# A selective scan's tiles laid out channel by channel, with the gate taken where the sums leave PSUM

## The chip, the core and the metric

The kernel runs on one core of a Trainium2 chip. The metric is the device time of one execution in microseconds. The core's engines have queues of their own: PE (TensorE, matmuls), DVE (VectorE), ACT (ScalarE), POOL (GpSimd) and SP (SyncE), which here issues nearly all DMA transfers. The profile counts 16 DMA engines.

## What is computed

The reference is a chain of four layers on an image batch of 4 x 128 channels x 64 x 64: an attention layer, an adder convolution layer, a gated attention with an MLP, and a Mamba-like layer. The change touches only the end of the last one. What it has to compute, cut from the reference:

```python
def _selective_scan(u, delta, A, Bm, Cm, Dv, z):
    dA = jnp.exp(jnp.einsum('bdl,dn->lbdn', delta, A))
    dBu = jnp.einsum('bdl,bnl,bdl->lbdn', delta, Bm, u)
    ...
        h = a * h + bu            # step by step along l
    ...
    y = jnp.einsum('lbdn,bnl->bdl', hs, Cm) + Dv[None, :, None] * u
    return y * _silu(z)

y_f = _selective_scan(xs, delta, A, Bm, Cm, D_param, z)
y_b = _selective_scan(flip(xs), flip(delta), A_b, flip(Bm), flip(Cm), D_param, flip(z))
y = y_f + flip(y_b)
mamba_out = jnp.einsum('bdl,od->blo', y, out_proj_w)
x_processed = _layer_norm(mamba_out, ln_w, ln_b)
...
return f_mamba + gamma * f_low
```

There are 256 channels `d`, 16 states `n`, and 4096 positions `l` an image; the recurrence runs once forward and once backward, with the same inputs.

## The kernel before, in words

The layers run one after the other. The last one has two functions. `layer3_prepare` computes, image by image, what the scan needs and writes it to memory tensors: `delta_d`, `du_d` (delta times u), `xs_d` (u), `sz_d` (silu of z), `low_d` (the gated low part) and `xdbl_d` (rows of B and C). `layer3_scan` reads these back.

**A tile** of the scan is 8 channels by 16 states on the 128 partitions; there are 4 images x 2 halves of the channels x 16 = 128 of them. A partition stands for one pair of channel and state. So each of the 8 rows of `delta_d` and `du_d` has to stand on 16 partitions, and each of the 16 rows of B and C on 8. The DMA does this with a repeated (zero-step) dimension in its source: `by_channels` (L921 to L926) loads `dl` and `du`, half an image's positions (2048) at a time; `by_states` (L908 to L919) loads B and C once an image and half. Before, the state is the slow index: partition = 8 x state + channel.

**Order within a tile** (`piece`, L936). Eight pieces of 1024 positions: e = 0 to 3 forward, e = 4 to 7 backward. For each, ACT computes `da` = exp(delta x A) into PSUM (L945) and DVE runs the recurrence (L947, one TENSOR_TENSOR_SCAN) into a buffer `h`. `dbu`, the scan's addend, is made by POOL from `du` and B (L933), one tile ahead.

**After the scan** of a tile, `merge` (L957) adds its forward and backward `h` on PE with identity matmuls into PSUM, in 8 blocks `mg` of 512; `copied` (L967) brings each to SBUF as `m` on ACT; `times_c` (L973) multiplies by C on POOL; `sums` (L977) adds over the 16 states on PE, with a matmul of `rows_of` that puts the tile's 8 channels on 8 of 32 rows, four tiles filling one PSUM tile `y`. After each fourth tile `evacuate` (L989) copies `y` out on ACT (L994) and stores it to `y_d` (L996), with the pattern [4, 32, 512] on the memory side.

**finish** (L998) takes one block of 512 positions of an image: it loads `y_d`, `xs_d` and `sz_d` for both channel halves (L1006), forms y + 2 D u by matmuls with the identity and with `skip` (L1008, L1009), gates on DVE (L1010), multiplies by the output weights on PE (L1014), takes the layer norm (Square on ACT, the mean on PE, then the root by a logarithm and an exponential on ACT, L68 and L69; the scale on DVE, L1023; the bias and the low part on POOL, L1024 and L1025), and stores `out` (L1026). 24 of the 32 blocks are finished in the loop, one at the end of every third tile; the last image's 8 come after the loop.

**What orders the work.** The loop at L1033 writes the calls in the order wanted, and a scheduling layer turns them into one instruction stream for each engine. Each engine takes its stream in order. Buffers come from pools with a fixed number each: 6 `h`, 3 `dl`, 2 `du`, 3 `dbu`, 2 `m`, 3 of B and of C, 2 PSUM tiles for `mg`, 2 for `da`. A load into a buffer stands in SP's queue until the last reader of that buffer is through, and what is behind it in the queue stands as well.

Of the kernel before, what the change touches and what calls it, by code (L numbers as in the profile page):

```python
# [16 lines left out]
P = 128  # L17
B = 4
# [812 lines left out]
def layer3_scan(  # L831
# [9 lines left out]
    with ExitStack() as ctx:  # L841
        cp = ctx.enter_context(tc.tile_pool(name="l4c", bufs=1))
        bc = ctx.enter_context(tc.tile_pool(name="l4bc", bufs=3))
# [6 lines left out]

        of8 = cp.tile([P, ND], F32, name="of8")
        nc.vector.tensor_reduce(of8, cm.ident.rearrange("p (n d) -> p d n", d=ND), AX.X, ALU.add)
# [5 lines left out]
        for j in range(4):  # L858
            nc.vector.tensor_copy(rows_of[:, j, ND * j : ND * (j + 1)], of8)

        a = []
        for name, src in (("af", a_log), ("ab", ab_log)):
# [5 lines left out]
            for c in range(2):  # L868
                spread = sb.tile([P, D_STATE, ND], F32, tag="spread", name=f"{name}_s{c}")
                nc.vector.tensor_tensor(  # L870
                    spread,
                    t[:, c, :].unsqueeze(2).broadcast_to([P, D_STATE, ND]),
                    of8.unsqueeze(1).broadcast_to([P, D_STATE, ND]),
                    ALU.mult,
                )
                pa = ps_m.tile([P, P // ND], F32, tag="mg", name=f"{name}_p{c}")
                nc.tensor.matmul(pa, spread.rearrange("p n d -> p (n d)"), group, start=True, stop=True)
                nc.vector.tensor_copy(at[:, c, :], pa)
            a.append(at)

        d2 = cp.tile([P, 2], F32, name="d2")
        nc.sync.dma_start(d2, d_param)

        nc.vector.tensor_scalar(d2, d2, 2.0, None, ALU.mult)
        skip = cp.tile([P, 2, P], F32, name="skip")
        for c in range(2):
            nc.vector.tensor_scalar(skip[:, c, :], cm.ident, d2[:, c : c + 1], None, ALU.mult)
# [20 lines left out]
        def by_states(b, h):  # L908

            if (b, h) not in by_image:  # L910
                got = []
                for what in range(2):
                    t = bc.tile([P, HL], F32, tag="BC"[what], name=f"{'BC'[what]}{b}_{h}")
                    r = DT_RANK + D_STATE * what
                    src = xdbl_d[b, r : r + D_STATE, halves[h]]
                    nc.sync.dma_start(t, src.unsqueeze(1).broadcast_to([D_STATE, ND, HL]))
                    got.append(t)
                by_image[b, h] = got
            return by_image[b, h]  # L919

        def by_channels(src, n, h, tag, bufs):  # L921
# [3 lines left out]
            nc.sync.dma_start(t, rows8.unsqueeze(0).broadcast_to([D_STATE, ND, HL]))  # L925
            return t  # L926

        def inputs(n, h):
# [4 lines left out]
            nc.gpsimd.tensor_tensor(t, du, by_states(b, h)[0], ALU.mult)  # L933
            st[n, "dbu", h] = t

        def piece(n, e):  # L936
# [3 lines left out]
            if k == way:  # L940
                st[n, way, h] = big.tile([P, HL], F32, tag="h", bufs=6, name=f"h{n}_{way}_{h}")
# [25 lines left out]
        def copied(n, e):  # L967
            h, k = block_of(e)
            if k == 0:
                st[n, "m", h] = big.tile([P, HL], F32, tag="m", bufs=2, name=f"m{n}_{h}")  # L970
            nc.scalar.copy(st[n, "m", h][:, bass.ts(k, BK)], st.pop((n, "mg", e)))  # L971

        def times_c(n, h):  # L973
            m = st[n, "m", h]
            nc.gpsimd.tensor_tensor(m, m, by_states(tiles[n][0], h)[1], ALU.mult)  # L975

        def sums(n, h):  # L977

            j = tiles[n][2] % 4
            if j == 0:  # L980
                st["y", h] = ps_y.tile([P, BK], F32, tag=f"y{h}", name=f"y{n}_{h}")
            m = st.pop((n, "m", h))
            for g in range(4):
                nc.tensor.matmul(  # L984
                    st["y", h][32 * g : 32 * g + 32, :], rows_of[:, j, :], m[:, bass.ts(g, BK)],
                    start=(j == 0), stop=(j == 3), skip_group_check=True,
                )

        def evacuate(n, h):  # L989
            b, c, i = tiles[n]  # L990
            if i % 4 < 3:
                return
            t = sb.tile([P, BK], F32, tag="ye", name=f"ye{n}_{h}")
            nc.scalar.copy(t, st.pop(("y", h)))  # L994
            r = 8 * (i - 3)
            nc.sync.dma_start(y_d[b, c, r : r + 32, halves[h]].rearrange("r (g w) -> g r w", g=4), t)  # L996

        def finish(b, k):  # L998
# [3 lines left out]
            gated = []  # L1002
            for c in range(2):
                yx = sb.tile([P, 3, BK], F32, tag="yx", name=f"yx{v}_{c}")
                for q, src in enumerate((y_d, xs_d, sz_d)):
                    nc.sync.dma_start(yx[:, q, :], src[b, c, :, ck])  # L1006
                py = ps_m.tile([P, BK], F32, tag="mg", name=f"py{v}_{c}")
                nc.tensor.matmul(py, cm.ident, yx[:, 0, :], start=True, stop=False)  # L1008
                nc.tensor.matmul(py, skip[:, c, :], yx[:, 1, :], start=False, stop=True)  # L1009
                nc.vector.tensor_tensor(yx[:, 0, :], py, yx[:, 2, :], ALU.mult)  # L1010
                gated.append(yx[:, 0, :])
            po = ps_m.tile([P, BK], F32, tag="mg", name=f"po3_{v}")
            for c in range(2):
                nc.tensor.matmul(po, ow[:, c, :], gated[c], start=(c == 0), stop=(c == 1))  # L1014
            sq = sb.tile([P, BK], F32, tag="sq4", bufs=1, name=f"sq4_{v}")
            nc.scalar.activation(sq, po, AF.Square)
            pv = ps_m.tile([P, BK], F32, tag="mg", name=f"pvo{v}")
            nc.tensor.matmul(pv, cm.mean, sq, start=True, stop=True)  # L1018
            rs = sb.tile([P, BK], F32, tag="rs4", bufs=1, name=f"rs4_{v}")
            cm.rstd(nc, rs, pv)  # L1020
            fl = sb.tile([P, BK], F32, tag="fl", name=f"fl{v}")
            nc.sync.dma_start(fl, low_d[b, :, ck])
            nc.vector.scalar_tensor_tensor(rs, po, lw, rs, ALU.mult, ALU.mult)  # L1023
# [180 lines left out]
```

## Time and profile before

| what | value |
|---|---|
| median of 3 runs | 23555.58 us (23554.83 to 23556.7) |
| the profiled execution | 23557.55 us, span 23555.8 us |
| scan stage, first `dl` load to end of the last scan | 20211.4 to 23424.2 us |
| one scan of 1024 positions (L947) | 2349 ns |
| `da` (L945) | 1118 ns |
| `dbu` (L933), `m` times C (L975), each on 2048 positions | 4529 ns, 4522 ns |
| `m` copy (L971) | 581 ns |
| `dl`, `du` loads | 256 each, 1024 KB each |

In a group line of the profile stand the line, engine and operation, the output and inputs, the shape and count; then the busy time and the mean of one in ns; then the engine's idle time just before, and what ended most of it. The busy digits cut the span into 40 slices and give each slice's busy share in tenths. In a line for a stretch of time there is the stretch and its length, then busy time and count of PE, PEld (weight loads), DVE, ACT and POOL, the granted TensorE clock, the mean busy share of the 16 DMA engines, and what they moved in GB/s. A line of waits names who waited for whom, with the total in us, the times, and the longest.

### The profile page before, as it was taken

What the parts mean: (1) busy time and instruction counts of PE and PEld (TensorE: products, weight loads), DVE (VectorE), ACT (ScalarE), POOL (GpSimd) and SP (SyncE); (2) the same over time, 40 slices, a digit from 0 to 9 for tenths busy, and PEclk for the clock granted to TensorE, in tenths of its full rate; (3) what the DMA queues carried; (4) which work ended last, traced back from release to release, by engine and by line L of the source; (5) the groups of instructions that cost most, each with busy time, mean ns of one, the idle gap of its engine ahead of it and who ended that gap; (6) DMA issues with size and microseconds to landing.
All of it is one profiled execution on the core that took longest, in us unless ns stands there. A gap on an engine that the chain in (4) does not pass through costs nothing. (4 is left out here: it accounts for less than half of the span.)

```text
span 23555.8 us, 348033 instructions
## 1 busy us (share of the span) xinstructions
PE 21606.2 (92%) x146624; PEld 7799.2 (33%) x146624; DVE 20116.0 (85%) x15018; ACT 19647.4 (83%) x13700; POOL 3766.7 (16%) x1710
## 2 busy tenths in 40 slices
PE   9999999999999999999999999999997567677777
PEld 4443333333333333333333333333332222222222
DVE  7887999999999999889999999999997665777776
ACT  5666999999999999899999999999996336555555
POOL 5662000000000000000000000000000000577776
PEclk9999999999999999999999999999998776899999
DMA  0000000000000000000000000000000002788876
GB/s 14 9 5 12 1 3 7 1 3 5 3 3 1 3 1 3 8 5 3 5 3 1 5 5 1 3 1 3 3 1 32 0 3 96 182 195 194 194 192 163
DMA packets 174504, 809.07 MB, mean 34 GB/s; under 512 B 22716, under 2 KB 23364, under 8 KB 102788
## 3 DMA queue, kind: packets, MB, share of 16 engines
q1 hardware_dynamic: 172356, 778.42, 13.0%
q8 instruction: 1146, 18.78, 0.3%
q10 hardware_dynamic: 576, 8.39, 0.1%
q14 instruction: 426, 3.49, 0.0%
HBM read 658.15 MB, written 128.58 MB: 33 GB/s over the span
## 5 line engine op out<-in xcount | busy, mean ns | idle before, releaser
L392 ACT ACTIVATE a1a<-a1pb,a1wn 128x2048 f32<-128x2048 f32 x4096 | 7793.2, 2001 | 198.3 <-PE a1pa L338 101.3
L392 ACT ACTIVATE a2a<-a2pb,a2wn 128x2048 f32<-128x2048 f32 x4096 | 7791.9, 1999 | 136.2 <-PE a2pa L338 94.0
L403 DVE TENSOR_SCALAR a2d<-a2pb,a2wa 128x2048 f32<-128x2048 f32 x4096 | 4993.4, 1281 | 212.9 <-PE a2pa L338 212.4
L403 DVE TENSOR_SCALAR a1d<-a1pb,a1wa 128x2048 f32<-128x2048 f32 x4096 | 4992.1, 1281 | 207.2 <-PE a1pa L338 206.9
L338 PE MATMUL a2pa<-a2a,a2pick 128*32 128x512 f32 x32768 | 4576.3, 593 | 31.5 <-ACT a2a L392 31.5
L338 PE MATMUL a1pa<-a1a,a1pick 128*32 128x512 f32 x32768 | 4569.2, 593 | 31.5 <-ACT a1a L392 31.5
L338 PE MATMUL a2pa<-a2d,a2pick 128*32 128x512 f32 x32768 | 4436.8, 594 | 46.3 <-DVE a2d L403 46.0
L338 PE MATMUL a1pa<-a1d,a1pick 128*32 128x512 f32 x32768 | 4434.3, 594 | 47.2 <-DVE a1d L403 46.9
L421 DVE SCALAR_TENSOR_TENSOR a1a<-a1pb,a1wa,a1a 128x2048 f32<-128x2048 f32 x1024 | 2406.1, 2350 | 323.6 <-ACT a1a L392 323.6
L421 DVE SCALAR_TENSOR_TENSOR a2a<-a2pb,a2wa,a2a 128x2048 f32<-128x2048 f32 x1024 | 2406.1, 2350 | 314.1 <-ACT a2a L392 314.1
L338 PEld LDWEIGHTS a2pa<-a2a,a2pick 128*32 128x32 f32 x32768 | 1489.1, 110 | 2370.1 <-issue 2061.7
L338 PEld LDWEIGHTS a1pa<-a1a,a1pick 128*32 128x32 f32 x32768 | 1486.9, 110 | 2370.7 <-issue 2045.3
L962 PE MATMUL mg<-h,ident 128*128 128x512 f32 x4096 | 1982.8, 634 | 298.1 <-ACT m L971 227.4
L338 PEld LDWEIGHTS a2pa<-a2d,a2pick 128*32 128x32 f32 x32768 | 1347.1, 109 | 2472.1 <-issue 1935.5
L338 PEld LDWEIGHTS a1pa<-a1d,a1pick 128*32 128x32 f32 x32768 | 1345.4, 109 | 2471.8 <-issue 1913.8
L947 DVE TENSOR_TENSOR_SCAN h<-da,h,dbu 128x1024 f32<-128x1024 f32 x768 | 1804.2, 2349 | 87.0 <-POOL dbu L933 4.7
L962 PEld LDWEIGHTS mg<-h,ident 128*128 128x128 f32 x4096 | 787.1, 201 | 1529.4 <-issue 856.9
L186 POOL TENSOR_TENSOR ssum<-ssum,et 128x512 f32<-128x512 f32 x960 | 1230.3, 1282 | 232.9 <-ACT et L181 166.1
L975 POOL TENSOR_TENSOR m<-m,C 128x2048 f32<-128x2048 f32 x256 | 1157.7, 4522 | 605.2 <-ACT m L971 435.9
L933 POOL TENSOR_TENSOR dbu<-du,B 128x2048 f32<-128x2048 f32 x256 | 1153.6, 4529 | 26.3 <-DMA du<-du_d 26.3
L151 ACT COPY et<-pe 128x512 f32<-128x512 f32 x1024 | 596.6, 583 | 591.6 <-PE pe L149 575.9
L149 PE MATMUL pe<-q,k 128*128 128x512 f32 x2048 | 1051.1, 596 | 8.6 <-DVE mx L159 8.1
(267 smaller groups left out, 13672.1 us busy)
## 6 DMA issues: line engine op xcount, KB each, us to landing
dl<-delta_d SPq DMA_DIRECT2D x256, 1024.0 KB
du<-du_d SPq DMA_DIRECT2D x256, 1024.0 KB
xs_d<-xs SPq DMA_DIRECT2D x8, 2048.0 KB
sz_d<-sz SPq DMA_DIRECT2D x64, 256.0 KB
delta_d<-dv SPq DMA_DIRECT2D x32, 512.0 KB
du_d<-du SPq DMA_DIRECT2D x32, 512.0 KB
y_d<-ye SPq DMA_DIRECT2D x64, 256.0 KB
yx<-xs_d SPq DMA_DIRECT2D x64, 256.0 KB
```

Of the source, the lines that this page charges most:

```text
L149: nc.tensor.matmul(pe, k[:, bass.ts(j, P)], unit[u, "q"], start=True, stop=True)
L151: nc.scalar.copy(et, pe)
L186: nc.gpsimd.tensor_tensor(unit[u, "sum"], unit[u, "sum"], at, ALU.add)
L338: nc.tensor.matmul(pa[s][32 * g : 32 * g + 32, :], pick[v][:, 31 - jj : 63 - jj], d[:, bass.ts(s, BK)], start=False, stop=False, skip_grou ...
L392: nc.scalar.activation(rows(at), view(t), AF.Abs, bias=wn[t][:, co : co + 1], scale=0.5 if g == q else 1.0,)
L403: nc.vector.tensor_scalar(rows(dt), view(t), wa[:, t, co : co + 1], None, ALU.max)
L421: nc.vector.scalar_tensor_tensor(at, view(MAX_TAP), wa[:, MAX_TAP, co : co + 1], at, ALU.max, ALU.add)
L933: nc.gpsimd.tensor_tensor(t, du, by_states(b, h)[0], ALU.mult)
L947: nc.vector.tensor_tensor_scan(t[:, cols][:, s], da[:, s], st[n, "dbu", h][:, cols][:, s], 0.0 if e % 4 == 0 else st["last"], ALU.mult, AL ...
L962: nc.tensor.matmul(pm, cm.ident, st[n, way, h][:, bass.ts(k, BK)], start=(way == 0), stop=(way == 1))
L975: nc.gpsimd.tensor_tensor(m, m, by_states(tiles[n][0], h)[1], ALU.mult)
```

## The change

1. The partitions are numbered the other way round: partition = 16 x channel + state. `by_channels` and `by_states` swap the place of the repeated dimension in the source, and the small constant matrices follow (`of16`, `spread`).
2. B and C are loaded one at a time and for the next image ahead (`next_image`), with 2 buffers each in place of 3.
3. There are 7 `h` buffers for 6 and 3 `m` buffers for 2. In the loop `times_c` and `sums` come later: half 0's product with C one step later, half 1's one step later, the sums of half 0 four steps and of half 1 three steps later.
4. The skip term and the gate move from `finish` to `sums` and `evacuate`. `xs` and `sz` are loaded in the layout of `y` (pattern [4, 32, 512], new L1005), the skip is added in PSUM by 32 x 32 matmuls (new L1016), and DVE multiplies by `sz` as it takes `y` out (new L1026). `y_d` then holds gated values.
5. `finish` is a generator that is stepped through at each even step of the loop. It loads only `y_d` and `low_d` (new L1035, L1037), adds the bias to `low` on ACT (new L1039), scales on ACT (new L1045), and multiplies and adds on POOL (new L1054, L1056). `gated`, `fl` and `mo` have one buffer each.
6. The table of ACT functions that has exponential and logarithm together is loaded once ahead of the stage.

```diff
-        bc = ctx.enter_context(tc.tile_pool(name="l4bc", bufs=3))
+        bc = ctx.enter_context(tc.tile_pool(name="l4bc", bufs=2))
...
+        of16 = cp.tile([P, ND], F32, name="of16")
+        nc.vector.tensor_reduce(of16, cm.ident.rearrange("p (d n) -> p d n", d=ND), AX.X, ALU.add)
...
+        tc.keep_in_program_order(nc.scalar.preload_act_table_set("natural_log_exp_and_others"))
...
-                    nc.sync.dma_start(t, src.unsqueeze(1).broadcast_to([D_STATE, ND, HL]))
+                nc.sync.dma_start(t, src.unsqueeze(0).broadcast_to([ND, D_STATE, HL]))
...
+        def next_image(n, what, h):
+            if n % 32 == 31:
+                by_states(tiles[n][0] + 1, what, h)
...
-            nc.sync.dma_start(t, rows8.unsqueeze(0).broadcast_to([D_STATE, ND, HL]))
+            nc.sync.dma_start(t, rows8.unsqueeze(1).broadcast_to([ND, D_STATE, HL]))
...
-                st[n, way, h] = big.tile([P, HL], F32, tag="h", bufs=6, name=f"h{n}_{way}_{h}")
+                st[n, way, h] = big.tile([P, HL], F32, tag="h", bufs=7, name=f"h{n}_{way}_{h}")
...
-                st[n, "m", h] = big.tile([P, HL], F32, tag="m", bufs=2, name=f"m{n}_{h}")
+                st[n, "m", h] = big.tile([P, HL], F32, tag="m", bufs=3, name=f"m{n}_{h}")
...
+        def blocks_of(t, n, h):
+            b, c, i = tiles[n]
+            r = 32 * (i // 4)
+            return t[b, c, r : r + 32, halves[h]].rearrange("r (g w) -> g r w", g=4)
...
+            if j == 1:
+                for name, src in (("xs", xs_d), ("sz", sz_d)):
+                    t = sb.tile([P, BK], F32, tag=name, bufs=2, name=f"{name}4_{n}_{h}")
+                    nc.sync.dma_start(t, blocks_of(src, n, h))
+                    st[name, h] = t
...
+            if j == 3:
+                for g in range(4):
+                    rows32 = slice(32 * g, 32 * g + 32)
+                    nc.tensor.matmul(
+                        st["y", h][rows32, :], skip[rows32, c, q, :], st["xs", h][rows32, :],
+                        start=False, stop=True, skip_group_check=True, tile_position=(32 * g, 32 * g),
+                    )
...
-            nc.scalar.copy(t, st.pop(("y", h)))
+            t = st.pop(("sz", h))
+            nc.vector.tensor_tensor(t, st.pop(("y", h)), t, ALU.mult)
+            nc.sync.dma_start(blocks_of(y_d, n, h), t)
...
+            gated = sb.tile([P, 2, BK], F32, tag="gated", bufs=1, name=f"gated{v}")
             for c in range(2):
-                yx = sb.tile([P, 3, BK], F32, tag="yx", name=f"yx{v}_{c}")
-                for q, src in enumerate((y_d, xs_d, sz_d)):
-                    nc.sync.dma_start(yx[:, q, :], src[b, c, :, ck])
...
+                nc.sync.dma_start(gated[:, c, :], y_d[b, c, :, ck])
+            fl = sb.tile([P, BK], F32, tag="fl", bufs=1, name=f"fl{v}")
+            nc.sync.dma_start(fl, low_d[b, :, ck])
+            yield
+            nc.scalar.activation(fl, fl, AF.Identity, bias=lb)
...
+            mo = sb.tile([P, BK], F32, tag="mo", bufs=1, name=f"mo{v}")
+            nc.scalar.activation(mo, po, AF.Identity, scale=lw)
...
-            nc.vector.scalar_tensor_tensor(rs, po, lw, rs, ALU.mult, ALU.mult)
-            nc.gpsimd.tensor_scalar(rs, rs, lb, None, ALU.add)
-            nc.gpsimd.tensor_tensor(fl, rs, fl, ALU.add)
+            nc.gpsimd.tensor_tensor(mo, mo, rs, ALU.mult)
+            yield
+            nc.gpsimd.tensor_tensor(fl, mo, fl, ALU.add)
             nc.sync.dma_start(out[b, :, ck], fl)
```

The loop's part, with the calls in their new places:

```diff
+            if n >= 36 and at % 3 == 0 and at // 3 < NB:
+                steps = finish(b - 1, at // 3)
...
-                    times_c(n - 2, 0)
...
+                if e == 1 and 1 < n:
                     times_c(n - 2, 0)
+                    sums(n - 2, 1)
                 if e == 2 and 1 < n:
-                    sums(n - 2, 0)
...
+                    evacuate(n - 2, 1)
+                if e == 5 and 0 < n <= last + 1:
+                    times_c(n - 1, 1)
+                if e == 6:
+                    if n < last:
+                        inputs(n + 1, 1)
+                    if 1 < n:
+                        sums(n - 2, 0)
+                if e == 7 and 1 < n:
                     evacuate(n - 2, 0)
...
+                if e % 2 == 0:
+                    next(steps, None)
```

## The prediction

> **What bounds the kernel now.** I read the slices first, then the stretches of the scan stage, the waits inside it, and last the DMA transfers alone. Only the scan (`layer3_scan`) changes. It runs from the first `dl` load at 20211.4 us to the end of the last scan at 23424.2 us: 3212.8 us for 128 tiles, **25.1 us a tile**, with 131.6 us of tail behind it. The rest of the run keeps its instructions.
>
> ```profile
> DVE  7887999999999999889999999999997665777776
> POOL 5662000000000000000000000000000000577776
> DMA  0000000000000000000000000000000002788876
> GB/s 14 9 5 12 1 3 7 1 3 5 3 3 1 3 1 3 8 5 3 5 3 1 5 5 1 3 1 3 3 1 32 0 3 96 182 195 194 194 192 163
> ...
> POOL dbu L933 1%; POOL m L975 1%; DVE h L947 0%; PE y L984 0%; PE mg L962 0%; PE po L1014 0%; POOL rs L1024 0%; POOL fl L1025 0%; PE py L1008 0%; ACT L69 0%; PE py L1009 0%; PE pvo L1018 0%; ACT rs L68 0%; ACT L68 0%; DVE rs L1023 0%
> ...
> L947 DVE TENSOR_TENSOR_SCAN h<-da,h,dbu 128x1024 f32<-128x1024 f32 x768 | 1804.2, 2349 | 87.0 <-POOL dbu L933 4.7
> L975 POOL TENSOR_TENSOR m<-m,C 128x2048 f32<-128x2048 f32 x256 | 1157.7, 4522 | 605.2 <-ACT m L971 435.9
> L933 POOL TENSOR_TENSOR dbu<-du,B 128x2048 f32<-128x2048 f32 x256 | 1153.6, 4529 | 26.3 <-DMA du<-du_d 26.3
> ```
>
> No engine is full in the last six slices, and the DMA digit is the highest there. The chain that ended last goes round POOL, DVE and PE. The waits of DVE between 20600 and 23400 us say which of them holds the scans:
>
> ```profile
> DVE h L947 <- PE mg L962: 432.2, 222, 4.7
> DVE rs L1023 <- ACT rs L69: 200.5, 24, 10.2
> ```
>
> So the scans stand 432 us for the merges to free an `h` buffer, and 200 us behind the layer norm's L1023, of 2800 us. They stand for a DMA nowhere. Yet the transfers are near their own limit. These stretches show it; the last two columns are the share of 16 DMA engines and GB/s:
>
> ```profile
> 20211.40:23424.20 3212.80, 2493.78 (x6433) 889.31 (x6434) 2434.17 (x1109) 1819.31 (x2223) 2353.70 (x557) 0.93 0.81 192
> ...
> 20214.00:20259.00 45.00, 15.13 (x24) 5.66 (x24) 26.33 (x16) 16.85 (x18) 19.02 (x5) 0.57 1.02 221
> 20046.00:20069.50 23.50, 14.24 (x23) 5.01 (x23) 5.33 (x11) 23.21 (x31) 0.00 (x0) 0.67 1.02 234
> 17952.00:17968.00 16.00, 1.06 (x2) 0.50 (x2) 11.67 (x4) 3.62 (x1) 0.00 (x0) 0.50 1.01 431
> 23442.50:23444.40 1.90, 0.00 (x0) 0.00 (x0) 0.69 (x1) 0.00 (x0) 1.90 (x1) 1.00 0.25 92
> ```
>
> The first is the stage: share 0.81. The second holds `dl` and `du` loads alone: all engines busy at 221 GB/s, 221/(16 x 1.02) = 13.5 GB/s for each. The third holds B and C loads alone: 14.3 each. The fourth holds loads of `x` from `y2d`, with no repeated rows: 26.7 each. The fifth is one `y_d` store (L996) alone: share 0.25, 92/4 = 23 GB/s each. **Four engines of sixteen carry it.** Its small completion packets say the same:
>
> ```profile
> DMA packets 124, 0.25 MB, mean 49 GB/s; under 512 B 4, under 2 KB 4, under 8 KB 124
> ```
>
> What sets that store apart is its access pattern: [4, 32, 512] on the memory side, its slowest dimension 4. The loads with all engines have 16 (`dl`: 16 repeats of 8 rows; B: 16 rows of 8 repeats) or 128 there.
>
> **Part by part.**
>
> *The h buffers, the later sums, the m buffers.* One more `h` buffer lets the first scan of a tile wait for the merge of two tiles before, half 1, instead of half 0, and each later one likewise; this can take the 432 us. The sums and products with C move past merges in PE's queue, so PE no longer stands for POOL there.
>
> *The gate and the layer norm.* L1010 (64 x 0.67 us) and L1023 (32 x 0.75) leave DVE, with the 200 us wait; the multiply by `sz` comes back at the sums (64 x 0.67). 64 table loads of 1.28 us leave ACT's finish; two Identity activations (0.6 us each, by the row of Square) come in; 64 copies `ye` (0.58) go. POOL swaps 1.57 + 1.27 us for 2 x 1.27 a finish. PE trades 128 `py` matmuls of 128 rows for 256 of 32 rows. On engines alone, a tile would come to 8 scans at 2.43 us (three take 7.29 in a row) plus 0.33 for the gate: 19.8; POOL 4 x 4.53 + 0.6 = 18.7. Call it **20.5 us**, worth about 590 us over 128 tiles if nothing else came late.
>
> *The layout of the loads.* This is what comes late. To put 8 channels by 16 states on the partitions, the `dl` and `du` loads (4 a tile, 1 MB each) now name [8 rows, 16 repeats, 2048], and B and C [8 repeats, 16 rows, 2048]: **the slowest dimension is 8 where it was 16**. No row has an 8. By the nearest row, the 4 that got four engines, I take eight. The other end is sixteen, as now.
>
> [...]
>
> On eight engines one load is 1,048,576/8 = 131,072 bytes each. At 14.3 GB/s (the B and C stretch, whose pattern gives each engine one row to repeat, as the new `dl` has) it takes 9.17 us; at 13.5, 9.7; at 26.7, 4.91. I take 9.17, the nearest row.
>
> [...]
>
> Then a tile costs the busiest DMA engine:
> - `dl`, `du`: 4 x 9.17 = 36.7 us
> - gate: the new `xs`, `sz` loads (4 in four tiles) have slowest dimension 4, as the 2 `y_d` stores: 65,536 bytes on each of four engines at 23 GB/s = 2.85 us; 6/4 x 2.85 = 4.3. This counts them on engines that also carry `dl`. If they fell on others it is 0; if the loads ran at half rate, 7.1
> - finish: 4 transfers of 16,384 bytes an engine at 26.7 GB/s, 0.6 us each, 32 finishes: 0.6
> - B and C: 12 loads in the loop, 0.9
>
> Sum **42.4 us**, against 20.5 for the engines. The cover is gone: scans now wait for `dl`. The loads are two or three deep in the queue (3 `dl`, 2 `du` buffers), 18 to 27 us of work, so DMA hardly runs dry. One place where it does: with one `fl` buffer, SP's next `fl` load stands until the `out` store has landed, and `dl` is queued behind it on SP. The store is the last thing in the queue then. The price of an emptied queue is about one small transfer, by the chain of waits:
>
> ```profile
> 23509.90 4.94 DMA fl<-low_d
> ```
>
> 24 finishes lie in the loop: 24 x 4.9 = 118 us. In the tail the last eight finishes go one by one with that buffer; I leave the tail at 131.6 us, the table loads going and the single buffer coming.
>
> 128 x 42.4 + 118 = 5545 us, against 3212.8: +2332. The profiled execution took 23557.6 us around its span of 23555.8, 2 us over the median, so this gives **25,890 us** (+9.9%).
>
> **The rivals.**
>
> *Eight engines, at full rate.* If half rate is a matter of sixteen engines and eight do not keep it, a load takes 4.91: 19.6 + 4.3 + 0.6 + 0.5 = 25.0 us a tile, 128 x 25.0 + 118 = 3318: 23,660 us, +0.4%. Anything between is open. For it: 26.7 occurs. Against: the half rate holds in two stretches whose sources are read in quite different order (13.5 and 14.3), so it does not hang on the order of the rows.
>
> *Sixteen engines as now; faster.* If the 8 does not lower the count, a load is 65,536 bytes each, 4.58 us at 14.3: 18.3 + 4.3 + 0.6 + 0.4 = 23.6 us, still over 20.5. 128 x 23.6 + 60 (half the dry spells, as engines catch up) = 3081: 23,425 us, -0.55%. It decides as soon as a tile's transfers fall under today's 25.1. For it: dl's destination keeps 128 partitions. Against: so does the store's SBUF side.
>
> *The high end.* At 13.5 GB/s and with the gate's loads at half rate: 38.7 + 7.1 + 0.6 + 0.9 = 47.3; 6054 + 118 = 6172: 26,520 us.
>
> **How the numbers follow.** Eight engines near half rate, 25,300 to 26,520: 0.78. Eight at a higher rate, 23,660 to 25,300: 0.12, of it 0.02 at the very bottom with no change to speak of. Sixteen: 0.07 (0.06 faster, 0.01 same). Above 26,520: 0.03. 0.2% (47 us) is about what a measurement of this kernel can tell from no change. Faster 0.06, same 0.03, slower 0.91. The range 23,660 to 26,520 takes in both bounds of the load's rate; the likeliest case's own is 25,300 to 26,520.
>
> **What would show it.** A stretch of the changed scan stage with a DMA share near 0.5 or a little over, and about 115 to 130 GB/s, not 0.81 and 192; a count of small completion packets near half for `dl` and `du`; ACT's `da` and POOL's `dbu` waiting for `dl` and `du` where they now wait for DVE; PE `mg` gone as the releaser of the scans; DVE under 60% busy. A share above 0.8 would prove me wrong on the count of engines. A share of 0.5 with some 200 GB/s would prove me wrong on the rate.

## The result, and the profile after

The changed kernel takes **24300.67 us** (median of 4 runs, 24293.83 to 24324.94) against 23555.21 us before (4 runs): ratio **1.0319, 95% interval 1.0302 to 1.0335**, slower. The forecast was 25,890 us. The profiled execution took 24324.94 us around a span of 24323.1 us.

First the slices of the profiled page, each digit a fortieth of the span:

```profile
DVE  7787999999999999899999999999976655656555
POOL 5661000000000000000000000000000014655555
DMA  0000000000000000000000000000000024444444
GB/s 15 8 5 11 1 6 3 1 3 6 1 3 1 3 3 1 12 1 3 6 1 3 5 3 3 1 3 3 1 31 0 4 101 140 174 149 162 152 160 140
```

The scan stage has grown from the last six slices to the last seven, its DMA digit has halved to 4, and DVE and POOL are down to 5 and 6. The digit 4 is not slack: the stretches say so. These are the stage, 45 us early in it (87 us after its start) with `dl` and `du` loads alone, and the tail; the last two columns are again the share of 16 DMA engines and GB/s:

```profile
20213.00:24219.00 4006.00, 2517.55 (x6712) 896.90 (x6713) 2403.48 (x1100) 1734.61 (x2158) 2348.74 (x557) 0.82 0.48 156
20300.00:20345.00 45.00, 24.60 (x53) 8.27 (x52) 25.37 (x11) 15.38 (x19) 20.47 (x5) 0.77 0.51 114
24219.00:24323.00 104.00, 64.10 (x145) 20.59 (x144) 1.60 (x3) 31.43 (x50) 35.56 (x20) 0.77 0.26 81
```

4006/128 = **31.3 us a tile** (25.1 before). A share of 0.5 is what eight engines of sixteen, always busy, come to; over the whole stage the queue of the loads has 48.3%. If all of that lay on the same eight, they were idle for 3.4% of the stage, some 140 us. The engines' work is what it was (POOL 2348.74 us against 2353.70 before). The stage waits for loads. The DMA transfers of the stage alone, in packets:

```profile
DMA packets 110565, 626.31 MB, mean 156 GB/s; under 512 B 6520, under 2 KB 6520, under 8 KB 43384
```

The packets under 512 B go with the share. One `y_d` store of before, at share 0.25, has 4 of them. The loads in the first 87 us of this stage, at share 0.50, have 71 in 9.52 MB, 7.8 a load of 1 MB; those in the first 89 us of before's stage, at share 1.00, have 288 in 19.50 MB, 15.5 a load:

```profile
DMA packets 1232, 9.52 MB, mean 109 GB/s; under 512 B 71, under 2 KB 71, under 8 KB 71
```

```profile
DMA packets 2667, 19.50 MB, mean 220 GB/s; under 512 B 288, under 2 KB 288, under 8 KB 288
```

The same view of before's whole stage counts 11784 against the 6520: the bytes are nearly the same (617.13 MB), the small packets little over half. The waits between 20600 and 24100 us:

```profile
DVE h L958 <- PE mg L973: 1088.2, 197, 43.5
PE mg L973 <- ACT m L982: 1041.8, 258, 29.8
ACT da L956 <- DMA dl<-delta_d: 1028.4, 104, 36.9
...
POOL mo L1054 <- ACT rs L69: 264.9, 24, 33.4
...
POOL dbu L943 <- DMA du<-du_d: 251.5, 47, 9.2
```

ACT stands 1028 us for `dl`. The two lines above it read as the same wait seen from behind: ACT takes its queue in order, the `mg` copies (L982) stand behind the `da` that lacks its `dl`, PE finds no PSUM buffer for the next merge, and the `h` buffer that DVE needs stays taken. The wait behind L1023 of before (DVE for ACT's root, 200 us) is gone from DVE, as the change meant; POOL, which now multiplies by the root, stands 264.9 us for it.

### The profile page after: what moved, and what is told of

Same layout as the page of the kernel before. It is cut to its first block, busy times and chain, and to the rows that moved or that the text cites. A ratio compares the mean times of both kernels' runs of the same rounds, so it can differ in the third digit from the quotient of the medians.

```text
span 24323.1 us, 348426 instructions
## 1 busy us (share of the span) xinstructions
PE 21606.6 (89%) x146880; PEld 7797.8 (32%) x146880; DVE 20072.1 (83%) x14994; ACT 19552.8 (80%) x13636; POOL 3760.8 (15%) x1710
## 4 chain that ended last, share of the span: by engine, by line
PE 74%; DMA 10%; DVE 7%; ACT 4%; issue 3%; POOL 1%; SPq 0%; DVEq 0%; ACTq 0%; POOLq 0%
PE a1pa L338 29%; PE a2pa L338 29%; DMA dl<-delta_d 6%; PE pe L149 4%; PE pav L192 3%; DVE h L958 2%; DVE g L652 2%; PE mg L973 1%; PE a1pc L319 1%; PE a2pc L319 1%; DMA du<-du_d 1%; DMA y_d<-sz 1%; POOL dbu L943 1%; PE pd L637 1%; DMA out<-fl 1%
## 5 line engine op out<-in xcount | busy, mean ns | idle before, releaser
L973 PE MATMUL mg<-h,ident 128*128 128x512 f32 x4096 | 2140.0, 670 | 1486.3 <-ACT m L982 1208.8
L956 ACT ACTIVATE da<-dl,af 128x1024 f32<-128x1024 f32 x512 | 571.9, 1119 | 1383.6 <-DMA dl<-delta_d 1211.7
```

Source lines behind the costliest of these rows:

```text
L973: nc.tensor.matmul(pm, cm.ident, st[n, way, h][:, bass.ts(k, BK)], start=(way == 0), stop=(way == 1))
```

## The experiments

### Which part costs the time: e1_old_layout, e2_layout_alone, e3_gate_split

**e1** takes the layout alone back out of the changed kernel (as well as the constants that follow it):

```diff
-                nc.sync.dma_start(t, src.unsqueeze(0).broadcast_to([ND, D_STATE, HL]))
+                nc.sync.dma_start(t, src.unsqueeze(1).broadcast_to([D_STATE, ND, HL]))
-            nc.sync.dma_start(t, rows8.unsqueeze(1).broadcast_to([ND, D_STATE, HL]))
+            nc.sync.dma_start(t, rows8.unsqueeze(0).broadcast_to([D_STATE, ND, HL]))
```

> The changed kernel with the layout alone taken back (state slow, 16 repeats x 8 rows, 16 rows x 8 repeats), all its other parts kept. Theory 1 (the loads' count of engines is what made the change slower): a tile's transfers on the busiest engine are 4 x 4.6 to 4.85 + 4.3 + 0.6 + 0.4 = 23.7 to 24.7 us, the stage about 3030 to 3160 us plus some dry spells, so 23,400 to 23,570 us; DMA share in the stage 0.75 to 0.85. Rival (the new order of the calls, the gate's loads or the one fl buffer made it slower): 24,200 to 24,300 us.

Measured: 23630.61 us, ratio 1.0026 (1.0015 to 1.0037): 60 us over theory 1's range, and far from the rival's. **e2** is the reverse edit, the layout alone put into the kernel before.

> The kernel before with the layout alone changed (8 rows x 16 repeats, 8 repeats x 16 rows), nothing else. Theory 1: on eight engines at the 0.40 us a packet that the changed kernel shows, a tile takes 64 x 0.40 = 25.8 us for dl and du, 1.4 for the y_d stores, 1.2 for finish and 0.9 for B and C: 29.3 us, against 25.1 now, so 23,555 + 128 x 4.2 = about 24,090 us, share 0.5. Rival (the layout costs nothing by itself): 23,555 us.

Measured: 23946.23 us, ratio 1.0162 (1.0145 to 1.0178), 144 us under theory 1's figure. A stretch of 2400 us of each, e1 first:

```profile
20600.00:23000.00 2400.00, 1733.58 (x4886) 610.23 (x4886) 1723.00 (x782) 1254.76 (x1563) 1700.67 (x404) 0.89 0.83 191
```

```profile
20600.00:23000.00 2400.00, 1682.32 (x4217) 583.51 (x4215) 1584.41 (x715) 1183.41 (x1454) 1543.38 (x366) 0.88 0.52 168
```

With the layout out, the share is 0.83; with the layout as the only edit it is 0.52. So the layout sets the share, and without it all the rest of the change costs 0.26%. The two do not add up: 0.26% and 1.62% apart, 3.19% together. What the rest costs seems to depend on whether loads are the bound.

**e3** takes the gate's transfers (loads of `xs` and `sz`, stores of `y_d`) apart, each into four of 32 rows (the cut shows the loads):

```diff
-                    nc.sync.dma_start(t, blocks_of(src, n, h))
+                    for g in range(4):
+                        nc.sync.dma_start(t[32 * g : 32 * g + 32, :], blocks_of(src, n, h)[g])
```

> The changed kernel with each xs and sz load and each y_d store cut into four transfers of 32 rows, so that their slowest dimension is 32 in place of 4. If these transfers run on engines that also carry dl and du (theory 1): 6/4 x 2.85 = 4.3 us of a tile becomes 6/4 x 4 x 4,096 bytes / 26.7 = 0.9, so 3.4 us x 128 = 435 us less, 23,870 us; the share rises to about 0.55. If they run on other engines: no change, 24,300 us. [...]

Measured: 25105.38 us, ratio 1.0652 (1.0634 to 1.067): 800 us over the higher of the two cases, and 1235 over theory 1. SP's waits between 20600 and 23000 us, where L1006 issues the split loads, and the same stretch:

```profile
SPq L1006 <- DMA du<-du_d: 337.1, 46, 9.4
SPq L1006 <- DMA dl<-delta_d: 315.6, 51, 9.7
```

```profile
20600.00:23000.00 2400.00, 1454.47 (x3375) 484.36 (x3375) 1201.91 (x543) 863.63 (x1072) 1172.52 (x276) 0.79 0.52 130
```

SP now stands at the split loads until earlier `dl` and `du` loads have landed, so the next ones are issued late. And at the same share of 0.52, the GB/s are 130 where the changed kernel had 156: an 8 KB packet takes 0.530 us on average (mean over the trace's records of 8 KB packets in the loads' queue, here and below) against 0.403. So the time of a packet is no constant of the pattern. **e6_old_split** puts the same split on e1:

> The changed kernel with the layout of before and its gate's transfers cut into four of 32 rows each, so that no transfer is left on fewer than sixteen engines. Theory 1: 4 x 4.75 + 0.9 + 0.6 + 0.4 = 20.9 us a tile of transfers, engines 20.5: with dry spells 21.5 to 23 us a tile, 23,070 to 23,260 us, faster than both kernels. [...] Rival (more issues on SP's queue, each standing for an earlier transfer, cost what the split saves): 23,600 us as in the run with the old layout alone.

Measured: 23804.73 us, ratio 1.0106 (1.0089 to 1.0123), slower than e1 and 200 us over the rival's figure. Its packets took 0.584 us, as e1's 0.582, so their length is not the reason here. The reason that the trace offers is the waits of SP's queue (261.5 us at the split loads for `du` between 20600 and 23000 us).

### The loads by themselves: e4_loads

> Loads alone, in eight phases of 18 loads issued in a row; the rest of the computation is left out and the output is not the reference's. Phases: a = 8 rows x 16 repeats on 128 partitions (the changed kernel's dl); b = 16 repeats x 8 rows (the dl of before); c = 16 rows x 8 repeats (the B of before); d = 8 rows x 8 repeats on partitions 0 to 63; e = 8 rows x 4 repeats on partitions 0 to 31; f = 4 rows x 16 repeats on partitions 0 to 63; g = 8 blocks of 16 different rows, nothing repeated; k = 128 different rows, nothing repeated. [...] Theory 2 (repeated reads of the same rows cause the half rate): g and k are at 310 from the start, e is as slow as a. Theory 3 (the number of engines does not follow the slowest dimension): shares near 1.0 in a, d, e, f, g.

This kernel only loads. The stretches of its eight groups, a to g and then k, in order of time (the last is 128 different rows; the last two columns are share and GB/s):

```profile
10.00:170.00 160.00, 0.00 (x0) 0.00 (x0) 1.00 0.51 111
180.00:255.00 75.00, 0.00 (x0) 0.00 (x0) 1.00 1.01 222
268.00:340.00 72.00, 0.00 (x0) 0.00 (x0) 1.00 1.01 230
352.00:428.00 76.00, 0.00 (x0) 0.00 (x0) 1.00 0.51 114
440.00:455.00 15.00, 0.00 (x0) 0.00 (x0) 1.00 0.51 214
470.00:550.00 80.00, 0.00 (x0) 0.00 (x0) 1.00 0.25 105
600.00:655.00 55.00, 0.00 (x0) 0.00 (x0) 1.00 0.51 213
665.00:705.00 40.00, 0.00 (x0) 0.00 (x0) 1.00 1.01 424
```

Two things are read here. **The share follows the slowest dimension**: 8 rows x 16 repeats, 0.51; 16 x 8 in either order, 1.01; 8 x 8 and 8 x 4, 0.51; 4 x 16, 0.25; 128 rows, 1.01. In the eight groups a slowest dimension of 4 goes with a quarter of the engines' time, 8 with half, 16 and 128 with all of it; theory 3 fails.

**The rate is not a matter of repeats alone.** The first group, the changed kernel's load, runs at 111 GB/s, 0.598 us a packet, from its first to its last load; the fourth, the same on 64 partitions, stays near 0.58 as well. The fifth repeats each row four times and runs at 214, 0.309 us; it fills only 32 partitions. So repeats are not enough to make a load slow. But they have a part in whether it stays slow. The seventh writes the partitions of the first, in the same eight blocks, from 128 different rows: it begins at 0.517 us and falls to 0.310 with nothing between its loads (the stretch shows it after the fall). On sixteen engines the second and third, with repeats, stay near 0.57 to 0.60, and the eighth, without, takes 0.31 after a slow beginning (0.343 us in its first eighth).

What makes a packet long or short is not shown. The traces name no engine and no partition for a packet. The first group on 128 partitions stays at 0.598 us and the fifth on 32 is at 0.309, both at share 0.51; but the fourth and the sixth both fill 64 partitions with repeated rows, and the fourth stays near 0.58 while the sixth fell to 0.31 by itself within its first quarter.

### What lets the packets fall: e10_step, e17_even_gate, e18_alone, e19_stores, e20_no_stores

The 0.403 us of the changed kernel is the mean of a mixture: 58% of the stage's 8 KB packets take under 0.345 us, against 8% in the kernel before. From 22050 to 22064 us no `dl` or `du` packet starts. From 22064 to 22072 us they take 0.470 us, from 22076 to 22091 us 0.366, and in the end (22087 to 22100 us) 0.316, at the same share:

```profile
22064.00:22072.00 8.00, 4.70 (x8) 2.10 (x9) 2.29 (x1) 3.80 (x6) 4.18 (x1) 0.59 0.52 148
22076.00:22091.00 15.00, 12.94 (x35) 4.90 (x36) 13.14 (x6) 10.09 (x13) 7.41 (x3) 1.00 0.51 180
```

It is so over the whole stage. There are 42 spells of over 1 us in which no 8 KB packet is under way, 264 us in all; packets that start within 10 us after such a spell take 0.54 us on the mean, those that start 40 us after it or later 0.37.

Which transfer makes the packets short? **e10** puts transfers between loads of the changed form:

> Loads alone again, the rest of the computation left out and the output not the reference's: seven phases of 18 loads (8 rows x 16 repeats, the changed kernel's dl, but phase d has 16 repeats x 8 rows) with something between. a = after each third load one load of the gate's kind ([4, 32, 512], four engines); b = after each third a plain load of 128 x 512 (sixteen engines); c = after each third the same bytes as a in four loads of 32 x 512 (sixteen engines each); d = as a, among the sixteen-engine loads of the layout before; e = after each third a store of the y_d kind (four engines); f = a single load of the gate's kind after the third; g = nothing between. [...] Theory 2 (a gap or any small transfer is enough): b and c fall as a does. Theory 3 (what is in the changed kernel comes from the memory side, the two tensors read in turn, not from small transfers): all stay near 598.

Measured, 8 KB packets in the first and the last sixth of a group: with the gate's form of load after each third load 0.574 to 0.320 us; with a plain 128 x 512 load 0.596 to 0.568; with four loads of 32 rows 0.601 to 0.334; with the old layout's loads and the gate's form 0.574 to 0.489; with the store of `y_d` 0.573 to 0.310; with one load of the gate's form near the front only, 0.578 all through; with nothing, 0.585. So not only the gate's forms shorten packets, since the split loads did it as well (0.334 us; no stretch holds loads of 32 rows alone, so their sixteen engines are an estimate), and one transfer of the gate's form was not enough (0.578). Theory 2 had b fall with c, and b hardly did. **e17** asks whether the gate's transfers, [4, 32, 512], are what keeps packets short in the kernel itself, and puts them into 128 rows:

```diff
-            r = 32 * (i // 4)
-            return t[b, c, r : r + 32, halves[h]].rearrange("r (g w) -> g r w", g=4)
+            x = (8 // len(halves)) * h + i // 4
+            return t[b, c, :, bass.ts(x, BK)]
```

> The changed kernel with the gate's loads of xs and sz and its store of y_d as blocks of 128 rows x 512 instead of 32 rows x 4 x 512 (the same bytes, on sixteen engines instead of four; the gate meets other values than it should, which is the part of the computation that this changes). [...] Rival (something else keeps the packets short, and the gate's transfers only add their 4.0 us a tile): packets stay at 0.38 to 0.43 us and the kernel takes 23,800 to 24,250 us, ratio 1.010 to 1.029.

Measured: 24229.27 us, ratio 1.0276 (1.0247 to 1.0306), packets 0.430 us. The rival holds, at the edge of its range: without transfers of the gate's form the packets did not go back to the 0.57 to 0.60 us of loads alone, so that form is not what keeps them short in the kernel. Both rates stand in e17's own trace at one share:

```profile
21940.00:21990.00 50.00, 26.56 (x71) 9.54 (x69) 27.80 (x12) 18.25 (x23) 30.09 (x7) 0.83 0.50 120
21800.00:21812.00 12.00, 11.44 (x29) 4.15 (x28) 11.26 (x6) 7.41 (x10) 7.48 (x2) 0.90 0.51 205
```

**e18** tries three differences between loads alone and loads in the kernel:

> Loads of the changed kernel's form alone (8 rows x 16 repeats, 1 MB), six groups of sixteen: a back to back from one tensor; b from two tensors in turn; c with DVE and POOL at work on other tiles; d with PE and ACT at work on other tiles; e one load let in only when the load two before it has landed and been read; f the same with DVE and POOL at work. (The kernel computes nothing of the reference; it only loads.) [...] Theory T (two sources): b alone falls. If none falls, what keeps the packets at 0.40 us in the kernel stays open.

Measured, mean packet of the six groups: 0.601, 0.587, 0.591, 0.580, 0.569, 0.569 us. None falls. The work of PE and ACT came later than meant, beside the fifth group and not the fourth, and did nothing there either. The groups with two loads in flight run at a share of 0.38, not at a shorter packet. **e19** asks which of the transfers that were left makes packets short among loads alone:

> Loads of the changed kernel's form (8 rows x 16 repeats, 1 MB), five groups of sixteen, with other transfers between them: a a store of 128 rows x 512 after every second load; b a load in the form of B (8 repeats x 16 rows, 1 MB) after every fourth; c a store and a load of 128 x 512 after every second; d a store of 128 x 512 and a load on four engines (32 rows x 4 x 512); e two loads in flight at most, with a load and a store of 128 x 512 after every second. (The kernel computes nothing of the reference; it only moves data.) [...]

Measured, by eighths of each group: a, with stores of 128 x 512, from 0.581 steadily down to 0.314 us; b, with loads in B's form, 0.572 to 0.575 and 0.587 at the end; c, store and load, 0.603 to 0.314; d from 0.578 with ups between to 0.326 in the seventh eighth and 0.402 in the last; e 0.521 to 0.362, mean 0.374. Among loads alone, stores are enough. Group a's beginning and end, and group b:

```profile
5.00:40.00 35.00, 3.77 (x3) 0.00 (x0) 1.00 0.54 127
100.00:128.00 28.00, 0.00 (x0) 0.00 (x0) 1.00 0.55 210
135.00:275.00 140.00, 0.34 (x1) 0.00 (x0) 1.00 0.51 115
```

**e20** then leaves every store out of e17's scan stage:

```diff
-            nc.sync.dma_start(blocks_of(y_d, n, h), t)
...
-                nc.sync.dma_start(gated[:, c, :], y_d[b, c, :, ck])
+                nc.sync.dma_start(gated[:, c, :], xs_d[b, c, :, ck])
...
-            nc.sync.dma_start(out[b, :, ck], fl)
```

> The changed kernel with the gate's transfers in 128 rows (24,229 us) and with no store at all in the scan stage: the store of y_d and the store of out are left out (the finish reads xs_d in place of y_d, and out is filled with ones at the kernel's start, so the last layer's result is not delivered). It moves 0.5 MB less for each half of four tiles. [...] Rival (the packets stay at 0.40 to 0.45 us and only the left-out work counts): 23,900 to 24,230 us, ratio 1.014 to 1.028.

Measured: 23728.99 us, ratio 1.0076 (1.0054 to 1.0098), packets 0.384 us: shorter than e17's 0.430, not longer, and the kernel faster than even the rival said. So stores are enough among loads alone and not needed in the kernel. The kernel is 500 us faster than e17; the shorter packets account for some 64 x 0.046 x 128 = 377 us of that (64 is the number of 8 KB packets on an engine in a tile). What the stores cost besides is in part in SP's queue. In e17 this line stands between 20600 and 23000 us, in e20 there is none:

```profile
SPq L1005 <- DMA y_d<-sz: 263.6, 21, 25.9
```

### What is left when the loads are fast: e8_after_plain, e9_before_plain

Both load `dl` and `du` from 128 different rows:

```diff
-            nc.sync.dma_start(t, rows8.unsqueeze(1).broadcast_to([ND, D_STATE, HL]))
+            nc.sync.dma_start(t, src[b, c, :, halves[h]])
```

> The changed kernel with its dl and du loads taken from 128 different rows, nothing repeated: the same bytes into the same tiles in the same order, on sixteen engines at about 314 ns a packet; the values are not the ones wanted, so the output is not the reference's. Theory 1 (the loads alone hold the changed kernel back): transfers come to 4 x 2.5 + 4.3 + 0.6 + 0.4 = about 15 us a tile, the engines' 20.5 us set the pace: 20,213 + 128 x 20.5 + 105 = 22,940 us. Rival (the later sums and products, the single fl buffer or the gate cost time by themselves): over 23,400 us.

> The kernel before with its dl and du loads taken from 128 different rows in the same way; the output is not the reference's. Theory 1 (before, the merges and the layer norm hold the scans, not the transfers): 23,500 to 23,560 us, a tile at 24.7 to 25.1 us. Rival (the transfers already set part of the pace): 23,300 us or less.

e8: 23422.34 us, ratio 0.9943 (0.9924 to 0.9963). e9: 23552.82 us, 0.9997 (0.9987 to 1.0008). So the kernel before was not held by its transfers, though their share was 0.81, and the changed one, with faster loads on sixteen engines (share 0.63 between 20600 and 23000 us; half of the packets take 0.309 us or less, the mean is 0.40), gains little of what it should: its theory 1 fails, its rival holds. In e8, undisturbed tiles follow each other at 19.8 us (scans of the first piece start at 21534.8, 21554.6 and 21574.4 us). 128 of those would take 2534 us; the stage took some 3100. About **570 us** are lost. The chain of waits and then SP's own timeline at one such place (start, duration):

```profile
21605.16 10.02 DMA out<-fl
21615.19 3.34 DMA fl<-low_d
```

```profile
21605.16 0.50 SPq L1056 DMA_DIRECT2D out<-fl  x1
21611.38 0.54 SPq L1004 DMA_DIRECT2D sz<-sz_d  x1
21615.19 0.31 SPq L1036 DMA_DIRECT2D fl<-low_d  x1
21615.60 0.86 SPq L934 DMA_DIRECT2D dl<-delta_d  x2
```

SP stands some 6 us before `sz`, then 3 before `fl`, which waits for `out` to land, and only then issues `dl`.

### Can that be had back: e11_bufs, e12_plain_bufs, e13_old_bufs, e15_plain_pool

The first three add a third `sz` buffer and a second `fl` buffer, to the changed kernel, to e8 and to e1:

```diff
-                    t = sb.tile([P, BK], F32, tag=name, bufs=2, name=f"{name}4_{n}_{h}")
+                    t = sb.tile([P, BK], F32, tag=name, bufs=3 if name == "sz" else 2, name=f"{name}4_{n}_{h}")
...
-            fl = sb.tile([P, BK], F32, tag="fl", bufs=1, name=f"fl{v}")
+            fl = sb.tile([P, BK], F32, tag="fl", bufs=2, name=f"fl{v}")
```

> The changed kernel with one buffer more for the gate's sz (3 instead of 2) and for fl (2 instead of 1); nothing else moves. Theory 1 (the loads of dl and du, sixteen 8 KB packets deep on each of eight engines, set the pace: 64 packets x 0.403 us = 25.8 us of a tile's 31.3): taking away part of SP's stalls gives only what of the 31.3 us isn't covered by packets, so 24,150 to 24,310 us, ratio 1.025 to 1.032, share of the DMA engines still 0.48 to 0.52. Rival (SP's stalls behind sz, y_d and fl cost the 550 to 570 us that the kernel with 128-row loads lost): 23,700 to 23,800 us, ratio 1.006 to 1.010.

> The kernel with dl and du loaded from 128 different rows (it reads other values in the scan, so its output is not the one wanted; same bytes), with the same two buffers more. It ran 23,422 us without them, some 568 us over 128 tiles x 19.8 us. If SP's in-order stalls (fl waiting for the store of out: 53 us; sz waiting for its last reader: 107 us; both listed over 2600 us of the stage) are what makes dl late, the buffers give 150 to 350 us back: 23,070 to 23,270 us, ratio 0.979 to 0.988. If the stall only moves to the next wait of the queue (y_d's store waiting for sz, out's store waiting for POOL), it stays at 23,380 to 23,430, ratio 0.993 to 0.995.

> The changed kernel with the layout of the states taken back (16 engines, 23,631 us without the buffers, 25.9 us a tile) and the same two buffers more. If SP's stalls are the rest of the loss there: 23,350 to 23,500 us, ratio 0.991 to 0.998, a kernel faster than both. If packets are (64 packets on 16 engines at some 0.6 us are 19 to 20 us of a tile, with the gate's four-engine transfers of 4.0 us beside or behind them): 23,580 to 23,630, ratio 1.001 to 1.003.

e11: 24388.17 us, 1.0347 (1.033 to 1.0364). e12: 23400.28, 0.9933 (0.9913 to 0.9953). e13: 23603.78, 1.0019 (1.0009 to 1.0028). The buffers give 16 to 27 us at most where the loads are on sixteen engines, with intervals that overlap those of e8 and e1, and nothing in the changed kernel, which came out 78 us over the top of theory 1's range. e12's waits of SP between 20600 and 23000 us have the same names as e8's:

```profile
SPq L1056 <- POOL fl L1055: 116.4, 16, 17.3
SPq L1026 <- DVE sz L1025: 97.8, 28, 5.5
```

The `out` store waits for POOL and the `y_d` store for DVE, and no buffer takes that away. **e15** moves the `fl` load and the `out` store of e12 to POOL's queue.

> The kernel with dl and du from 128 different rows and the two buffers more (23,400 us), with the finish's load of fl and store of out issued from POOL's queue instead of SP's (the scan reads other values than it should). If SP's in-order queue is what the 550 us are (out's store and fl's load stand 10.2 and 3.4 us in the chain of waits, and dl behind them): 22,950 to 23,200 us, ratio 0.974 to 0.985. If the wait goes to another transfer of that queue (sz for y_d's store) or to POOL: 23,350 to 23,450, ratio 0.991 to 0.996.

Measured: 23539.41 us, 0.999 (0.9979 to 1.0), slower than e12 and over both ranges. The wait has moved: ACT now stands 152.3 us for `fl` between 20600 and 23000 us (17.3 in e12), and still 287.2 us for `dl` (348.8 in e12). SP's in-order queue was not all of it; where the 570 us go has not been settled.

### A version faster than both: e14_gate_in_finish, e16_finish_pool

e14 keeps the change's order (seven `h`, three `m`, later sums and products, layer norm off DVE), with the old layout, and with the gate and the skip back in `finish`, whose loads have 128 rows:

```diff
-            t = st.pop(("sz", h))
-            nc.vector.tensor_tensor(t, st.pop(("y", h)), t, ALU.mult)
+            t = sb.tile([P, BK], F32, tag="ye", name=f"ye{n}_{h}")
+            nc.scalar.copy(t, st.pop(("y", h)))
...
+                for q, src in enumerate((y_d, xs_d, sz_d)):
+                    nc.sync.dma_start(yx[:, q, :], src[b, c, :, ck])
```

> The changed kernel's order of work (products with C and sums a step later, seven buffers of h, layer norm off VectorE) with the layout of the states taken back and the gate and the skip back in the finish, where their loads have 128 rows and the sums' way out of PSUM is ScalarE's copy. If the gate at the way out of PSUM is what costs the rest (its transfers on four engines, and sz and xs queued before dl): 23,150 to 23,350 us, ratio 0.983 to 0.991, the fastest of the set. If the finish's in-order stalls are (fl, out): 23,500 to 23,650, ratio 0.998 to 1.004.

> The changed kernel's order of work with the old layout and the gate in the finish (23,319 us), with fl and out on POOL's queue. There dl was late only 83.6 us in 2400, so SP's queue has little left to give: theory 1 says 23,230 to 23,330 us, ratio 0.986 to 0.990; if POOL, which the scans wait for, pays for issuing: 23,340 to 23,500, ratio 0.991 to 0.998.

e14: **23318.88 us, 0.9898 (0.9883 to 0.9913)**, 240 us under the kernel before beside it and the fastest here that does all the work. e16, with `fl` and `out` on POOL's queue: 23466.38 us, 0.9957 (0.9941 to 0.9974), in the range of the case where POOL pays. The trace puts it otherwise: ACT stands 201.5 us for `fl` between 20600 and 23000 us, against 67.3 in e14. In e14's waits between 20600 and 23000 us, `dl` is late by 83.6 us, against e1's 476.0:

```profile
ACT da L953 <- DMA dl<-delta_d: 83.6, 26, 8.9
```

So the order of work is worth having (23.3 us a tile), and the gate at the way out of PSUM cost about 300 us (e1 against e14, by their ratios). Whether that is its transfers on four engines or their place ahead of `dl` in SP's queue, these two runs do not separate.

## Why the prediction was right in direction and wrong in size

**The step that failed** is "I take 9.17, the nearest row", the time of one `dl` or `du` load on eight engines. It carried the rate of loads on sixteen engines (14.3 GB/s for each) over to loads on eight, for the whole stage. Loads of the new form alone do run at that rate (111 GB/s on eight engines is 13.9 each, e4), and early in the stage they did (114 GB/s). The prediction chose 14.3 over 13.5 because B's pattern would give each engine one row; no trace shows which engine reads which row. Over the stage a packet took 0.403 us, so a load of 16 packets on each engine took 16 x 0.403 = **6.45 us**. The prediction's own sum with this term is 4 x 6.45 + 4.3 + 0.6 + 0.9 = 31.6 us a tile, against 31.3 measured. With each run's own packet time the sum also comes near e17 (64 x 0.430 + 2.4 = 29.9 against 30.4) and e20 (64 x 0.384 + 1.95 = 26.5 against 26.6), with 0.6 us for each 128 x 512 transfer in place of the gate's term, and e2 (64 x 0.395 + 1.4 + 1.2 + 0.9 = 28.8 against 28.5), e11 (64 x 0.418 + 5.8 = 32.6 against 32.2) and e3 (64 x 0.530 + 2.4 = 36.3 against 37.4). The packet times are read from these runs, so this shows which term was off and not why.

Point by point:

- **Eight engines**: right. The share (0.50 at the start of the stage), the small packets (7.8 a load against 15.5) and e4 (0.51 for 8 rows x 16 repeats) show it; the prediction had it as an estimate from one store's four. The rival "sixteen engines" is out.
- **The rate**: wrong, and between the two bounds, as the rival "eight engines, at full rate" left open. The argument against that rival was that half rate does not hang on the order of the rows. That is so (e4, second and third group: 222 and 230 GB/s), but the rate is no constant either: the same form takes 0.598 us a packet alone and 0.403 in the stage. Rows from late in the kernel before would have given the same price: its packets took 0.566 us on the mean over the whole scan stage, 8% of them under 0.345. The old form hardly left the slow rate in the kernels, the new one did (58%), and no row of before shows the new form.
- **The gate's term, 4.3 us**: the sum needs it, but e17, which takes the four-engine transfers away, came out only 71 us faster, since its packets were longer (0.430 us). The term by itself was not measured.
- **The engines alone, 20.5 us**: about right; e8's undisturbed tiles take 19.8. The hidden gain existed, and e14 shows 240 us of it.
- **The dry spells, 118 us**: in the changed kernel, some 140 us of idle eight-engine time by the share; by the packet records 264 us without a large load under way, part of it filled by the gate's and the finish's transfers. But once loads are fast, e8 loses about 570 us to waits of which this one is a part. This term would have sunk the fast rivals: "sixteen engines" put 23.6 us a tile, and e1, which is that case, took 25.9 (from 20213 to 23526 us).
- **The tail, 131.6 us**: it shrank to 104.
- **What would show it**: share, the count of small packets, `da` and `dbu` waiting for their loads came as said. GB/s (156, not 115 to 130) showed the rate wrong. "PE `mg` gone as the releaser" was wrong in form: DVE still stands 1088.2 us for PE `mg`, which by the reading above is ACT's wait of 1028.4 us for `dl` under another name.

**What stays open** is why packets in the kernel are 0.38 to 0.43 us. Out as the sole cause are the gate's pattern (e17) and the stores (e20). Not enough alone are other engines' work, two sources, a short queue (e18), a plain load, or B's form (e10, e19). In four kernels' traces fewer spells of over 1 us without a large load go with shorter packets: 2 and 0.384 us in e20, 25 and 0.395 in e2, 42 and 0.403 in the changed kernel, 81 and 0.530 in e3. But e17 and e11 have 42 as well, with 0.430 and 0.418, and loads issued one behind the other stay at 0.598 all through (e4). So a cause is not shown.

## What to carry to other kernels

Before a layout moves to another partition order, count the slowest dimension of each repeated load: here 16 to 8 halved the engines' share (1.01 to 0.51 in e4) and made the loads the bound (ACT stood 1028.4 us for `dl`), in a kernel whose engines had less work. A rate taken from one access pattern is not a safe price for another, even where it held for a whole stage: here the old form took 0.566 us a packet and the new one 0.403. A run of the new loads alone would have misled too (0.598 us); only with other transfers between them did they speed up. Look also at what stands ahead of large loads in an in-order queue: taking the gate's transfers away from there (e14) went with some 300 us, though moving two others to POOL's queue made things slower (e15, e16).

## What the runs showed of the hardware

Loads of 1 MB on eight engines, into the same partitions, ran at 111 GB/s with rows repeated sixteen times and, after a slow beginning, at 213 with different rows (e4, first and seventh group): 0.598 against 0.310 us for a packet of 8 KB. The slow form stays slow for 160 us of such loads alone. With stores of 128 x 512, or with loads of 32 rows, between them, packets come down to 0.31 to 0.33 us within some 130 to 140 us (e19, e10), and the same queue then moves 210 GB/s in place of 115. The old layout has the same half rate on sixteen engines: 222 and 230 against 424 GB/s with 128 different rows. e9 shows that the kernel before would not have gained from the full rate (ratio 0.9997).
